# Two graph layers on one core: layer 0's T built transposed and unnormalized, its four second-set PSUM banks made one tile

## The chip, the cores and the metric

The kernel runs on one core of a Trainium2 chip. All data are fp32. The metric is the device time of one execution in microseconds. Engines are called PE (TensorE), DVE (VectorE), ACT (ScalarE), POOL (GpSimd) and SP (SyncE, which here only issues DMAs).

## The reference

Two layers work on 128 graphs of 128 nodes with 512 features. Layer 0, for each graph, with h = relu(layernorm(x)):

```python
Xw = X @ Wv + bv
sj = Xw @ aw[:d, 0]
si = Xw @ aw[d:, 0]
e = leaky_relu(sj[:, None, :] + si[:, :, None] + ab[0], negative_slope=0.2)
alpha_matrix = A * exp(e)
transition = alpha_matrix / (sum(alpha_matrix, axis=-1, keepdims=True) + 1e-12)
H = zeros; Xk = X
for k in range(3):
    H = H + Xk @ Wk[k] + bk[k]
    Xk = einsum('bij,bjd->bid', transition, Xk)
return relu(H)          # x = x + this
```

The kernel writes this as H = Y0 + T (Y1 + T Y2), with Yk = X Wk and T the transition matrix of the graph.

Layer 1, again on relu(layernorm(x)), forms q and k by one weight matrix, agg = adj k, a score per node from q and agg, a softmax of the scores over the nodes, and adds the softmax times X Wv1 to x.

## The kernel before, in words

**Pairs.** Layer 0 treats two graphs at a time (G = 2): 64 pairs p. The two graphs are the two block rows of one Strassen-Winograd product, so each product X W of a pair takes seven block products (`strassen`, L361) instead of eight. They run in the order P1, P5, P6, P2, P7, P3, P4, each of two accumulating matmuls, on four PSUM banks a, b, c, e. ACT copies one bank into another to seed the next accumulation (b<-a after P1, c<-b after P6) or into a buffer s (after P5 and P7). DVE adds s to a bank for the results e + s and b + s.

**Two bank sets.** PSUM has eight banks, each a tile of its own (L79): set1 = a1, b1, c1, e1, set2 = a2, b2, c2, e2 (L81). `y10` (L501) works on set1 and forms [Y1 | Y0] of pair p with 512 columns per matmul. `y2` (L427) works on set2 and forms Y2 of pair p + 2 with 257 columns, of which one is an attention column (si or sj).

**One pair in the loop (L644).** PE's order is written by hand: `ordered` (L88) chains every matmul to the one before. It is y10(p); inside it, after P6, two transposes of T(p) into a2 (`t_transposed`, L482); then `inner` (L514), four matmuls of 256 columns that add T Y2 onto the Y1 halves of the four set1 banks, each followed by an ACT copy of the sum to zz; then `outer` (L524), four matmuls of 256 columns that add T times that onto the Y0 halves; then y2(p + 2). DVE finishes with max(bank, 0) + x for each of the four blocks (L533), which goes to DRAM as x1d.

**T.** `attention` (L453) builds, on DVE and ACT, z = exp(leaky relu(sums of the two columns)), multiplies by the adjacency tile ag with a row sum (L466), adds 1e-12, takes the reciprocal and scales (L472). ag is loaded by SP (L107). A second copy of the adjacency matrix, agb, is loaded blockwise by POOL (L111) and transposed on DVE to aT (L475), times the mask, for layer 1.

**What else shares the queues.** For layer 1, DVE transposes h2 (`for_layer1`, L403) and, in every second pair, forms four sums (L420 to L424) that POOL's queue writes out (L422, L425). POOL's queue also carries the small pzd and pz DMAs of `y2` (L443, L445). `norm0`, `begin` and `norm2` make the layernorms and the left factors of coming pairs; `norm2_statistics(p)` runs behind product 2 of y2(p + 2).

**Order on the other engines.** A framework derives the waits between engines from the tiles that instructions read and write, and places DVE's, ACT's, POOL's and SP's instructions by its own plan of the times. `behind` (L83) keeps an instruction from being placed before a named earlier one.

**Layer 1** (L705 on) works on quads of four graphs, 32 in all. `together` (L809) alternates: product i on set1, product i on set2, product i + 1 on set1, and so on, with 2 + 2 factors and then 2 + 1; four matmuls on a1, a2, e1, e2 for `aggregate` (L879) stand in between. Its evacuations are like those of layer 0 (`one_round`, L741; `plain_ends`, `adding_ends`).

Of the kernel before, what the change touches and what calls it, by code (L numbers as in the profile page):

```python
# [16 lines left out]
def kernel(  # L17
# [60 lines left out]

    a1, b1, c1, e1, a2, b2, c2, e2 = (psum.tile([P, D], FP, name=n) for n in  # L79
                                      ("a1", "b1", "c1", "e1", "a2", "b2", "c2", "e2"))  # L80
    set1, set2 = (a1, b1, c1, e1), (a2, b2, c2, e2)  # L81
# [14 lines left out]

    xg, ag, agb = {}, {}, {}

# [4 lines left out]
    def load_adj(p):  # L103

        s = slice(p * G, (p + 1) * G)
        ag[p] = loads.tile([P, G, N], FP, name="ag", bufs=3)
        nc.sync.dma_start(ag[p], adj[s].rearrange("b n m -> n b m"))  # L107
        agb[p] = loads.tile([P, G, Q, S32], FP, name="agb", bufs=2)
        v = adj[s].rearrange("g (q b) (c i) -> c b (g q) i", b=S32, i=S32)
        for c in range(Q):  # L110
            nc.gpsimd.dma_start(agb[p][c * S32:(c + 1) * S32].rearrange("p g q i -> p (g q) i"), v[c])  # L111
# [21 lines left out]
    wkt = setup.tile([P, DC, D], FP, name="wkt")  # L133
    aw_bc = setup.tile([P, 2, D], FP, name="aw_bc")
    awr = t10[0:1, 2].rearrange("p c o -> p (c o)")
# [86 lines left out]
    def attention_columns():  # L222

        for f in range(DC):
            for a in range(2):
                junk = front.tile([P, D], FP, name="junk", bufs=1)
                done["u"] = nc.vector.scalar_tensor_tensor(
                    junk, wv0_sb[:, f], 1.0, aw_bc[:, a, :], op0=OP.mult, op1=OP.mult, accum_out=r2[:, f, a * (W2 + HD):a * (W2 + HD) + 1]).ins

# [81 lines left out]

    HV, LEFT, Y2, PZ, T, TT, X1, HV2, FW = ({} for _ in range(9))

# [89 lines left out]
    def for_layer1(p):  # L403

        q, second = divmod(p, 2)
        if not second:
            FW[q] = left.tile([P, 8, G, HC, N], FP, name="fw")
        f = FW[q]
        blocks, hv = f[:, L21:SLOT[4] + 1] if second else f[:, 0:SLOT[2] + 1:2], HV2.pop(p)
        for j in range(G):  # L410
            for k in range(2):
                nc.vector.transpose(blocks[:, k, j].rearrange("p f (n b) -> p f n b", n=Q),
                                    hv[:, j].rearrange("p n (k f a) -> p k f n a", k=2, f=HC)[:, k])
        if second:
# [9 lines left out]
            done["c12"] = nc.vector.tensor_sub(at[3], at[2], at[6]).ins  # L424
            queue.dma_start(fd[:, 4:].rearrange("p o n -> p (o n)"), fv[:, 4:].rearrange("p o n -> p (o n)"))  # L425

    def y2(p, steps={}, gate=None):  # L427


        add = partial(behind, gate, nc.vector.tensor_add) if gate else nc.vector.tensor_add  # L430
        y = Y2[p] = front.tile([P, G, 2, WP], FP, name="y2")[:, :, :, :W2]
        s = front.tile([P, 2, WP * 2], FP, name="s", bufs=1)[:, :, :W2]
# [20 lines left out]
    def attention(p, early_work=None):  # L453

        a, y, pz = ag.pop(p), Y2[p], PZ.pop(p)
# [8 lines left out]
        d = small.tile([P, 2, G], FP, name="d")  # L464
        for j in range(G):
            nc.vector.scalar_tensor_tensor(z[:, j, :], z[:, j, :], 1.0, a[:, j, :], op0=OP.mult,  # L466
                                           op1=OP.mult, accum_out=d[:, 0, j:j + 1])
        nc.vector.tensor_scalar(d[:, 0], d[:, 0], 1e-12, None, op0=OP.add)
        nc.vector.reciprocal(d[:, 1], d[:, 0])
        t = T[p] = front.tile([P, G, N], FP, name="t", bufs=1)  # L470
        for j in range(G):
            done["t"] = nc.vector.tensor_scalar(t[:, j, :], z[:, j, :], d[:, 1, j:j + 1], None,  # L472
                                                op0=OP.mult).ins
        aT = front.tile([P, G, N], FP, name="aT", bufs=1)
        nc.vector.transpose(aT.rearrange("p g n -> p (g n)"),  # L475
                            agb.pop(p).rearrange("p g q i -> p (g q i)"))
        for j in range(G):
            b = p * G + j
            behind("z", nc.scalar.activation, aT[:, j, :], aT[:, j, :], AF.Copy, scale=maskT[:, b:b + 1])
        nc.sync.dma_start(ATD[p], aT)  # L480

    def t_transposed(p):  # L482

        t, tt = T.pop(p), front.tile([P, G, N], FP, name="tt", bufs=1)
        pt = a2[:, :G * N].rearrange("p (g n) -> p g n", g=G)
        for j in range(G):
            ordered(nc.tensor.transpose, pt[:, j, :], t[:, j, :], ident)
        nc.scalar.copy(tt, pt)
        TT[p] = tt

# [7 lines left out]

    blocks1 = [(0, 0, a1), (1, 1, e1), (0, 1, b1), (1, 0, c1)]

    def y10(p, steps):  # L501

        s = front.tile([P, 2, WP * 2], FP, name="s", bufs=1)[:, :, :D]

        def end12(b, t):
            done["c12"] = behind("rs" if p else "t", nc.vector.tensor_add, b, b, t).ins

        strassen(set1, LEFT.pop(p), right10, s, False, {
            (0, 0): lambda a: None,
            (1, 1): lambda e, t: behind("rs" if p else "t", nc.vector.tensor_add, e, e, t),  # L510
            (0, 1): end12,
            (1, 0): lambda c: None}, steps, "warm" if p else "z")

    def inner(p):  # L514

        y = Y2.pop(p)
        z = front.tile([P, G, 2, HD], FP, name="zz", bufs=1)
        for j, nh, bank in blocks1:
            ordered(nc.tensor.matmul, bank[:, :HD], TT[p][:, j, :], y[:, j, nh, 1 - nh:W2 - nh], start=False,
                    stop=True, skip_group_check=True)  # L520
            nc.scalar.copy(z[:, j, nh], bank[:, :HD])
        return z

    def outer(p, z):  # L524

        tt, xs = TT.pop(p), xg.pop(p)
        hb = X1[p] = front.tile([P, G, D], FP, name="x1")
        for j, nh, bank in blocks1:
            ordered(nc.tensor.matmul, bank[:, HD:], tt[:, j, :], z[:, j, nh], start=False, stop=True,
                    skip_group_check=True)  # L530
        for j, nh, bank in blocks1:
            at = slice(nh * HD, (nh + 1) * HD)
            done["x1"] = nc.vector.scalar_tensor_tensor(hb[:, j, at], bank[:, HD:], 0.0, xs[:, j, at],  # L533
                                                        OP.max, OP.add).ins
        nc.sync.dma_start(X1D[p].rearrange("g n d -> n g d"), hb)
# [108 lines left out]
    for p in range(NP):  # L644
# [16 lines left out]
        if p > 1:  # L661
            behind("rs2", attention, p)
        y10(p, {1: between, 6: lambda: t_transposed(p)})
        if p > 0:
# [29 lines left out]
        if p == 3 + len(FACTORS):  # L694
# [415 lines left out]
```

## Time and profile before

| | us |
|---|---|
| median of 3 runs | 2298.38 |
| fastest, slowest of them | 2295.79, 2299.22 |
| span of the profiled execution | 2296.6 |
| layer 0 with its start, about | 0 to 1488 |
| layer 1, about | 1488 to 2296.6 |
| one pair of layer 0 (half of 687.96 to 732.51) | 22.27 |

The profile gives the span of the profiled execution, from its first to its last instruction; no other time of that execution is given, and the median lies 1.8 us above the span. In the timeline a line has the start in us, the length in us, the engine, the source line, the operation, what it writes and reads, and how many instructions are merged into it; in brackets stands how long the engine was idle before and what ended that. One fp32 matmul of the program appears as two MATMUL records, and their ends are modelled and overlap the next start, so that the distance between starts is what one takes. PEld is the weight load that goes ahead of a matmul.

### The profile page before, as it was taken

The numbers are of one execution on the slowest core, as the hardware profiler recorded it, in microseconds if no ns is written. First come the engines' busy times: TensorE is split into PE (matmuls) and PEld (weight loads), VectorE is DVE, ScalarE is ACT, GpSimd is POOL, SyncE is SP. The second block draws the span as 40 slices with busy tenths as digits, with TensorE's granted clock in tenths as the row PEclk, the third lists the DMA queues.
The fourth block names the chain that finished last, engine by engine and source line by source line (L and its number), as shares of the span: only waits on it lengthen the run. The fifth ranks groups of instructions, "written<-read, shape, count | busy, mean of one in ns | idle before, by whom it ended". The sixth has DMA issues, their size and how long they took to land.

```text
span 2296.6 us, 28967 instructions
## 1 busy us (share of the span) xinstructions
PE 2234.1 (97%) x8227; PEld 1547.1 (67%) x8227; DVE 1625.1 (71%) x4463; ACT 1273.3 (55%) x2933; POOL 699.6 (30%) x827
## 2 busy tenths in 40 slices
PE   9899999999999999999999999999999999999997
PEld 5565656566666656666565666578888888888885
DVE  5677767777677677767767776567777776776777
ACT  4455545555555555555555555356666666666665
POOL 3012111211212121121212112135555555555554
PEclk9999999999999999999999999999999999999999
DMA  8587786766766666676666667567888888888886
GB/s 228 161 261 218 240 243 212 219 211 195 237 200 213 223 208 214 196 236 197 211 228 203 217 198 224 186 242 225 246 234 231 240 231 229 249 232 231 246 237 190
DMA packets 343503, 507.78 MB, mean 221 GB/s; under 512 B 33178, under 2 KB 198426, under 8 KB 326958
## 3 DMA queue, kind: packets, MB, share of 16 engines
q1 hardware_dynamic: 302060, 382.40, 52.5%
q0 software_dynamic: 40992, 123.00, 20.1%
q8 instruction: 65, 1.06, 0.2%
q14 instruction: 96, 0.79, 0.1%
q10 hardware_dynamic: 290, 0.53, 0.1%
HBM read 289.62 MB, written 216.18 MB: 220 GB/s over the span
## 4 chain that ended last, share of the span: by engine, by line
PE 84%; DVE 6%; DMA 4%; ACT 4%; issue 2%; SPq 0%; POOL 0%; DVEq 0%; ACTq 0%; POOLq 0%
PE a L91 26%; PE c L91 23%; PE b L91 21%; PE e L91 13%; ACT h L306 2%; DVE z L466 1%; DMA rw<-rwd 1%; ACT s L86 1%; DMA pw<-pwd 1%; DMA h2d<-h 1%; DMA hd<-h 0%; DMA pwd<-pwt 0%; ACT z L463 0%; DMA tl<-in_L_gnn_Wqk_dram 0%; DVE t L472 0%
## 5 line engine op out<-in xcount | busy, mean ns | idle before, releaser
L111 POOL DMA_DIRECT2D agb<-in_adj_dram x256 | 150.2, 591 | 543.0 <-DVE aT L475 521.5
L570 POOL TENSOR_TENSOR c<-s,c 128x512 f32<-128x512 f32 (+1 forms) x186 | 199.7, 1088 | 257.9 <-DVE s L570 253.1
L91 PE MATMUL a<-r,x 128*128 128x512 f32 x512 | 243.4, 598 | 3.3 <-ACT a L493 3.2
L91 PE MATMUL b<-rw,in 128*128 128x256 f32 x896 | 215.0, 379 | 0.0
L91 PEld LDWEIGHTS b<-rw,in 128*128 128x128 f32 x896 | 170.6, 190 | 23.3
L289 DVE TENSOR_TENSOR r<-r 128x2 f32<-128x2 f32 x128 | 20.6, 161 | 214.6 <-ACT r L288 214.6
L386 ACT COPY s<-c 128x257 f32<-128x257 f32 (+1 forms) x128 | 61.4, 480 | 188.0 <-PE c L91 187.9
L570 POOL TENSOR_TENSOR c<-c 128x1024 f32<-128x1024 f32 (+1 forms) x70 | 152.2, 2184 | 13.6 <-DVE c L570 13.3
L91 PEld LDWEIGHTS a<-r,x 128*128 128x128 f32 x512 | 94.3, 195 | 68.9 <-issue 62.0
L378 ACT COPY b<-a 128x257 f32<-128x257 f32 (+1 forms) x128 | 59.4, 464 | 133.7 <-PE a L91 132.8
L91 PE MATMUL a<-w,x 128*128 128x257 f32 x512 | 132.0, 380 | 1.0 <-DVE x L338 1.0
L91 PE MATMUL b<-w,sx 128*128 128x257 f32 x512 | 132.0, 380 | 0.0
L443 POOL DMA_DIRECT2D pzd<-pzt x62 | 36.9, 595 | 281.4 <-DVE pzt L86 275.7
L91 PE MATMUL b<-t,sx 128*128 128x512 f32 x256 | 120.5, 593 | 1.0 <-ACT b L378 1.0
L91 PE MATMUL c<-t,x 128*128 128x512 f32 x256 | 120.4, 593 | 1.1 <-ACT s L386 1.1
L91 PE MATMUL c<-t,sx 128*128 128x512 f32 x256 | 121.3, 597 | 0.0
L91 PE MATMUL e<-t,sx 128*128 128x512 f32 x256 | 121.3, 596 | 0.0
L91 PE MATMUL b<-r,sx 128*128 128x512 f32 x256 | 120.3, 592 | 0.0
L570 DVE SCALAR_TENSOR_TENSOR junk<-agg,wscale,c 128x512 f32<-128x512 f32 x128 | 97.9, 765 | 31.4 <-POOL c L570 25.8
L570 ACT ACTIVATE c<-c,wcol 128x512 f32<-128x512 f32 x125 | 87.1, 719 | 59.4 <-DVE wcol L570 57.7
L306 ACT ACTIVATE h<-xg,rs 128x512 f32<-128x512 f32 x128 | 97.2, 807 | 37.5 <-DVE rs L294 36.5
L91 PE MATMUL c<-rw,in 128*128 128x256 f32 x448 | 109.1, 383 | 2.7 <-ACT c L570 2.6
(248 smaller groups left out, 5296.0 us busy)
## 6 DMA issues: line engine op xcount, KB each, us to landing
fd<-fw POOLq DMA_DIRECT2D x62, 1024.0 KB, 6.9
x1d<-x SPq DMA_DIRECT2D x64, 512.0 KB, 3.6
h2d<-h SPq DMA_DIRECT2D x64, 512.0 KB, 2.9
hv<-h2d SPq DMA_DIRECT2D x256, 128.0 KB, 4.3
f<-fd SPq DMA_DIRECT2D x32, 1024.0 KB, 6.1
xg<-in_x_dram SPq DMA_DIRECT2D x63, 512.0 KB, 4.8
hd<-h SPq DMA_DIRECT2D x63, 512.0 KB, 2.8
hv<-hd SPq DMA_DIRECT2D x252, 128.0 KB, 3.2
```

Source lines behind the costliest of these rows:

```text
L86: return op(*args, **how)
L91: done["mm"] = op(*args, **how).ins
L111: nc.gpsimd.dma_start(agb[p][c * S32:(c + 1) * S32].rearrange("p g q i -> p (g q) i"), v[c])
L289: nc.vector.tensor_mul(r[:, 2], r[:, 1], r[:, 1])
L306: nc.scalar.activation(to, at, AF.Relu, bias=rs[:, 1, j:j + 1], scale=rs[:, 0, j:j + 1])
L378: nc.scalar.copy(b, a)
L386: done["s7"] = nc.scalar.copy(s[:, 1], c).ins
L443: nc.gpsimd.dma_start(d.rearrange("g q b -> q g b"), t[::S32])
L466: nc.vector.scalar_tensor_tensor(z[:, j, :], z[:, j, :], 1.0, a[:, j, :], op0=OP.mult, op1=OP.mult, accum_out=d[:, 0, j:j + 1])
L570: done[engine] = op(*args, **how).ins
```

## The change

- The four banks of set2 become slices of one tile `banks2` of four banks. set1 stays four tiles.
- T is built transposed and without division: t = z times aT on DVE, directly in the layout that a matmul needs. The adjacency tile ag, its DMA, `t_transposed` with its two PE transposes and the ACT copy of T are gone. The attention columns of Y2 swap their places for it (index 1 - a).
- Y2 lies in two fixed buffers filled with ones at the start. The 257th column in front of `inner` is such a column of ones, so that T Y2 brings the row sums with it.
- `inner` writes to set2, starts new sums there, and stands behind P7 of y10 instead of behind P4.
- y10's four results go to a buffer yk in SBUF, by ACT copies for (0,0) and (1,0), which before stayed in PSUM, and by the DVE adds.
- `denominators` (DVE, two small operations) takes the row sums out of PSUM; `inner_out` (DVE, two operations of 512) divides T Y2 and adds Y1.
- `outer` is two matmuls of 512 columns to b1 and c1. u = bank / sum + Y0 is made by DVE, relu by ACT, the addition of x by POOL.
- The sums for layer 1 become a step of their own behind u. agb has three buffers, `stage` one.

```diff
-    a1, b1, c1, e1, a2, b2, c2, e2 = (psum.tile([P, D], FP, name=n) for n in
-                                      ("a1", "b1", "c1", "e1", "a2", "b2", "c2", "e2"))
+    a1, b1, c1, e1 = (psum.tile([P, D], FP, name=n) for n in ("a1", "b1", "c1", "e1"))
+    banks2 = psum.tile([P, 4, D], FP, name="banks2")
+    a2, b2, c2, e2 = (banks2[:, i] for i in range(4))
     set1, set2 = (a1, b1, c1, e1), (a2, b2, c2, e2)
...
-        ag[p] = loads.tile([P, G, N], FP, name="ag", bufs=3)
-        nc.sync.dma_start(ag[p], adj[s].rearrange("b n m -> n b m"))
-        agb[p] = loads.tile([P, G, Q, S32], FP, name="agb", bufs=2)
+        agb[p] = loads.tile([P, G, Q, S32], FP, name="agb", bufs=3)
...
+    y2s = [wpool.tile([P, G, 2, WP], FP, name=f"y2_{i}") for i in range(2)]
+    for t in y2s:
+        nc.gpsimd.memset(t, 1.0)
...
-        for j in range(G):
-            nc.vector.scalar_tensor_tensor(z[:, j, :], z[:, j, :], 1.0, a[:, j, :], op0=OP.mult,
-                                           op1=OP.mult, accum_out=d[:, 0, j:j + 1])
-        nc.vector.tensor_scalar(d[:, 0], d[:, 0], 1e-12, None, op0=OP.add)
-        nc.vector.reciprocal(d[:, 1], d[:, 0])
-        t = T[p] = front.tile([P, G, N], FP, name="t", bufs=1)
-        for j in range(G):
-            done["t"] = nc.vector.tensor_scalar(t[:, j, :], z[:, j, :], d[:, 1, j:j + 1], None,
-                                                op0=OP.mult).ins
...
+        t = TT[p] = front.tile([P, G, N], FP, name="t")
+        done["t"] = nc.vector.tensor_mul(t, z, aT).ins
...
-        for j in range(G):
-            ordered(nc.tensor.transpose, pt[:, j, :], t[:, j, :], ident)
-        nc.scalar.copy(tt, pt)
...
+        def add(j, nh, bank, t):
+            done["c12"] = behind(gate, nc.vector.tensor_add, to(j, nh), both(bank), both(t)).ins
+            if nh == j:
+                behind("c12", denominators, p)
+
+        strassen(set1, LEFT.pop(p), right10, s, False, {
+            (0, 0): lambda a: nc.scalar.copy(to(0, 0), both(a)),
+            (1, 1): partial(add, 1, 1),
+            (0, 1): partial(add, 0, 1),
+            (1, 0): lambda c: nc.scalar.copy(to(1, 0), both(c))}, steps, "warm" if p else "z")
+
+    def inner(p):
+
+        Y2.pop(p)
+        y = y2s[p % 2].rearrange("p j h o -> p (j h o)")
+        for i in range(4):
+            j, nh = divmod(i, 2)
+            n = D if p == NP - 1 and i in (1, 2) else W2
+            at = i * WP + 1 - nh
+            ordered(nc.tensor.matmul, set2[i][:, :n], TT[p][:, j, :], y[:, at:at + n], start=True, stop=True)
+
+    def denominators(p):
+
+        d = DEN[p] = small.tile([P, 2, G], FP, name="d")
+        nc.vector.tensor_scalar(d[:, 0], banks2[:, 0::2, HD], 1e-12, None, op0=OP.add)
+        nc.vector.reciprocal(d[:, 1], d[:, 0])
+
+    def inner_out(p):
+
+        z = Z[p] = y2s[p % 2][:, :, :, :HD]
+        for j in range(G):
+            done["c12"] = nc.vector.scalar_tensor_tensor(z[:, j], banks2[:, 2 * j:2 * j + 2, :HD], DEN[p][:, 1, j:j + 1],
+                                           yk[:, j, 0], op0=OP.mult, op1=OP.add).ins
...
+        for j, bank in enumerate((b1, c1)):
+            ordered(nc.tensor.matmul, bank.rearrange("p (h o) -> p h o", h=2), tt[:, j, :], z[:, j], start=True, stop=True)
+        us = [yk[:, j, 1].rearrange("p h o -> p (h o)") for j in range(G)]
+        for j, (u, bank) in enumerate(zip(us, (b1, c1))):
+            done["u0"] = nc.vector.scalar_tensor_tensor(u, bank, d[:, 1, j:j + 1], u, op0=OP.mult, op1=OP.add).ins
+            nc.scalar.activation(u, u, AF.Relu)
+            done["x1"] = nc.gpsimd.tensor_add(hb[:, j], u, xs[:, j]).ins
...
-        y10(p, {1: between, 6: lambda: t_transposed(p)})
+        y10(p, {1: between, 7: lambda: inner(p)})
+        behind("c12", inner_out, p)
...
-        z = inner(p)
...
-        behind("c12" if p else "left", outer, p, z)
+        behind("c12" if p else "left", outer, p)
+        if p > 0:
+            behind("u0", sums_for_layer1, p - 1)
...
-            stage = stage_ctx.enter_context(tc.tile_pool(name="stage", bufs=2, side="right"))
+            stage = stage_ctx.enter_context(tc.tile_pool(name="stage", bufs=1, side="right"))
```

More of the change, by code (lines that the diff above doesn't have):

```diff
@@ L95, in bcast @@
         return bass.AP(tensor=ap.tensor, offset=ap.offset + offset, ap=[[0, P], [1, n]])
-    xg, ag, agb = {}, {}, {}
+    xg, agb = {}, {}
     def load_x(p, queue=nc.sync):
@@ L133 @@
     wkt = setup.tile([P, DC, D], FP, name="wkt")
-    aw_bc = setup.tile([P, 2, D], FP, name="aw_bc")
+    yk = wpool.tile([P, G, 2, 2, HD], FP, name="yk")
+    aw_bc = yk[:, 0].rearrange("p k h o -> p k (h o)")
+    junk = yk[:, 1, 0].rearrange("p h o -> p (h o)")
     awr = t10[0:1, 2].rearrange("p c o -> p (c o)")
@@ L225, in attention_columns @@
             for a in range(2):
-                junk = front.tile([P, D], FP, name="junk", bufs=1)
                 done["u"] = nc.vector.scalar_tensor_tensor(
-                    junk, wv0_sb[:, f], 1.0, aw_bc[:, a, :], op0=OP.mult, op1=OP.mult, accum_out=r2[:, f, a * (W2 + HD):a * (W2 + HD) + 1]).ins
+                    junk, wv0_sb[:, f], 1.0, aw_bc[:, a, :], op0=OP.mult, op1=OP.mult, accum_out=r2[:, f, (1 - a) * (W2 + HD):(1 - a) * (W2 + HD) + 1]).ins
     def attention_constant():
@@ L310, in unpermuted @@
         return h.rearrange("p (f c a) -> p c f a", c=DC, f=Q)
-    HV, LEFT, Y2, PZ, T, TT, X1, HV2, FW = ({} for _ in range(9))
+    HV, LEFT, Y2, PZ, TT, DEN, Z, X1, HV2, FW = ({} for _ in range(10))
+    y2s = [wpool.tile([P, G, 2, WP], FP, name=f"y2_{i}") for i in range(2)]
+    for t in y2s:
+        nc.gpsimd.memset(t, 1.0)
     H2D, ATD, X1D = ([dram.tile(shape, FP, name=f"{name}{p}", bufs=1) for p in range(NP)]
@@ L413, in for_layer1, with sums_for_layer1 @@
                                     hv[:, j].rearrange("p n (k f a) -> p k f n a", k=2, f=HC)[:, k])
+    def sums_for_layer1(p):
+        q, second = divmod(p, 2)
         if second:
@@ L423, in for_layer1 @@
             nc.vector.tensor_sub(at[7], at[1], fv[:, L21])
-            done["c12"] = nc.vector.tensor_sub(at[3], at[2], at[6]).ins
+            nc.vector.tensor_sub(at[3], at[2], at[6])
             queue.dma_start(fd[:, 4:].rearrange("p o n -> p (o n)"), fv[:, 4:].rearrange("p o n -> p (o n)"))
@@ L430, in y2 @@
         add = partial(behind, gate, nc.vector.tensor_add) if gate else nc.vector.tensor_add
-        y = Y2[p] = front.tile([P, G, 2, WP], FP, name="y2")[:, :, :, :W2]
+        y = Y2[p] = y2s[p % 2][:, :, :, :W2]
         s = front.tile([P, 2, WP * 2], FP, name="s", bufs=1)[:, :, :W2]
@@ L453, in attention @@
     def attention(p, early_work=None):
-        a, y, pz = ag.pop(p), Y2[p], PZ.pop(p)
+        y, pz = Y2[p], PZ.pop(p)
         z = front.tile([P, G, N], FP, name="z", bufs=1)
@@ L463, in attention @@
         done["z"] = nc.scalar.activation(z, z, AF.Exp).ins
-        d = small.tile([P, 2, G], FP, name="d")
-        for j in range(G):
-            nc.vector.scalar_tensor_tensor(z[:, j, :], z[:, j, :], 1.0, a[:, j, :], op0=OP.mult,
-                                           op1=OP.mult, accum_out=d[:, 0, j:j + 1])
-        nc.vector.tensor_scalar(d[:, 0], d[:, 0], 1e-12, None, op0=OP.add)
-        nc.vector.reciprocal(d[:, 1], d[:, 0])
-        t = T[p] = front.tile([P, G, N], FP, name="t", bufs=1)
-        for j in range(G):
-            done["t"] = nc.vector.tensor_scalar(t[:, j, :], z[:, j, :], d[:, 1, j:j + 1], None,
-                                                op0=OP.mult).ins
         aT = front.tile([P, G, N], FP, name="aT", bufs=1)
@@ L480, in attention @@
         nc.sync.dma_start(ATD[p], aT)
-    def t_transposed(p):
-        t, tt = T.pop(p), front.tile([P, G, N], FP, name="tt", bufs=1)
-        pt = a2[:, :G * N].rearrange("p (g n) -> p g n", g=G)
-        for j in range(G):
-            ordered(nc.tensor.transpose, pt[:, j, :], t[:, j, :], ident)
-        nc.scalar.copy(tt, pt)
-        TT[p] = tt
     def seed_a():
@@ L497, in seed_e, with to, both @@
         nc.scalar.copy(e1, bias_e.rearrange("p k o -> p (k o)"))
-    blocks1 = [(0, 0, a1), (1, 1, e1), (0, 1, b1), (1, 0, c1)]
     def y10(p, steps):
         s = front.tile([P, 2, WP * 2], FP, name="s", bufs=1)[:, :, :D]
-        def end12(b, t):
-            done["c12"] = behind("rs" if p else "t", nc.vector.tensor_add, b, b, t).ins
+        gate = "rs" if p else "t"
+        def to(j, nh):
+            return yk[:, j, :, nh]
+        def both(bank):
+            return bank.rearrange("p (k o) -> p k o", k=2)
@@ L508, in y10 @@
+        def add(j, nh, bank, t):
+            done["c12"] = behind(gate, nc.vector.tensor_add, to(j, nh), both(bank), both(t)).ins
+            if nh == j:
+                behind("c12", denominators, p)
         strassen(set1, LEFT.pop(p), right10, s, False, {
[L509 to L512, printed above, removed]
+            (0, 0): lambda a: nc.scalar.copy(to(0, 0), both(a)),
+            (1, 1): partial(add, 1, 1),
+            (0, 1): partial(add, 0, 1),
+            (1, 0): lambda c: nc.scalar.copy(to(1, 0), both(c))}, steps, "warm" if p else "z")
@@ L514, in inner @@
     def inner(p):
[L516 to L526, printed above, removed]
-        hb = X1[p] = front.tile([P, G, D], FP, name="x1")
[L528 to L534, printed above, removed]
+        Y2.pop(p)
@@ new lines, in inner_out, with outer @@
+    def inner_out(p):
[3 more added lines that the diff above has]
+                                           yk[:, j, 0], op0=OP.mult, op1=OP.add).ins
+    def outer(p):
+        tt, xs, d, z = TT.pop(p), xg.pop(p), DEN.pop(p), Z.pop(p)
+        hb = X1[p] = front.tile([P, G, D], FP, name="x1")
+        for j, bank in enumerate((b1, c1)):
[5 more added lines that the diff above has]
+            done["x1"] = nc.gpsimd.tensor_add(hb[:, j], u, xs[:, j]).ins
@@ L680 @@
         if p == 0:
-            behind("x1", norm0, 3)
+            behind("u0", norm0, 3)
             setup_ctx.close()
@@ L702 @@
     for_layer1(NP - 1)
+    sums_for_layer1(NP - 1)
     def left1(q, o, i):
```

## The prediction, written before the changed kernel was run

> **What bounds the kernel now.** I read the page's engine shares first, then the chain that ended last, then two stage windows, then the timeline of one pair.
>
> ```profile
> span 2296.6 us, 28967 instructions
> PE 2234.1 (97%) x8227; PEld 1547.1 (67%) x8227; DVE 1625.1 (71%) x4463; ACT 1273.3 (55%) x2933; POOL 699.6 (30%) x827
> PE 84%; DVE 6%; DMA 4%; ACT 4%; issue 2%; SPq 0%; POOL 0%; DVEq 0%; ACTq 0%; POOLq 0%
> ```
>
> TensorE is the bound, and the stage windows (two pairs of layer 0; two quads of layer 1) say how tightly:
>
> ```profile
> core 0: us, PE busy (x) PEld busy (x) DVE busy (x) ACT busy (x) POOL busy (x), PEclk, DMA share, GB/s
> 687.96:732.51 44.55, 43.83 (x150) 27.61 (x149) 31.71 (x103) 23.86 (x56) 8.13 (x14) 1.00 0.68 212
> 1666.00:1715.67 49.67, 49.67 (x216) 40.71 (x215) 36.50 (x72) 31.34 (x70) 27.59 (x23) 1.00 0.81 234
> ```
>
> A pair of layer 0 takes 22.27 us with about 0.35 us of it idle on PE, a quad of layer 1 24.5 us with none. So whatever makes PE wait is added in full. Why it hardly waits today is seen in the timeline of one second-set product, Y2:
>
> ```profile
> 707.99 1.03 PE L91 MATMUL a<-w,x 128*128 128x257 f32 x4
> 708.86 1.03 PE L91 MATMUL e<-w,sx 128*128 128x257 f32 x4
> 709.05 0.36 ACT L378 COPY b<-a 128x257 f32<-128x257 f32 x1 [2.22 <-PE a L91]
> 709.72 1.03 PE L91 MATMUL b<-w,sx 128*128 128x257 f32 x4
> ```
>
> Products start 0.867 us apart. The copy out of bank a starts 0.19 us after P1's slot ended and lies wholly under the product into bank e. The one steady stall is at the transposes that the change removes:
>
> ```profile
> 720.09 0.52 PE L91 MATMUL a<-ident,t 128*128 128x128 f32 x2 [0.72 <-DVE t L472]
> 720.45 1.88 PE L91 MATMUL a<-r,x 128*128 128x512 f32 x4
> ```
>
> The two transposes hold PE for 0.36 us (720.09 to 720.45); over the kernel the list of waits counts 26.3 us in 31 waits of PE for t.
>
> **What the Trainium skill says.** "PSUM — Partial Sum Buffer", section "PSUM bank collisions raise a hardware error", asks that PSUM be guarded by bank and quadrant, and says that accesses to different banks run clean; so a wait between different banks is not asked for by the chip. "Perfetto Trace Analysis", section "Matmuls", wants matmul groups to rotate through banks so that the evacuation of one overlaps the next group; the four lines above agree (copy at 709.05 to 709.41 under 708.86 to 709.72). "TensorE: Matmul & The Clock Gate", section on the clock gate, says that an idle PE drops to half clock; the trace agrees once: after a wait of 3.20 us at 1468.58 two 512-wide products took 2.50 and 2.73 us instead of 1.72. Waits of 0.98 and 1.59 us early in the trace were followed by full-speed products.
>
> **The decisive edit: one tile for four banks.** The second set becomes slices of one tile `banks2`. I compared the two built programs instruction by instruction, with the semaphores that each waits for. In before, Y2's seven products wait for an evacuation three times (P6, P7, P4), each with a product in between as cover. In after, P5, P6, P2, P7, P3 and P4 all wait, each for the copy or add that reads the bank written just before it, though their own bank is another:
>
> ```
> product, bank     after waits for           before waits for
> P5  e2            ACT copy b2<-a2           nothing
> P6  b2            ACT copy s<-e2            ACT copy b2<-a2
> P2  a2            ACT copy c2<-b2           nothing
> P7  c2            ACT copy y<-a2            ACT copy c2<-b2
> P3  b2            DVE add y<-e2,s           nothing
> P4  c2            DVE add y<-b2,s           ACT copy s<-c2
> ```
>
> Nothing lies between product and evacuation any more. The price of such a wait is in before's start-up, where ACT was late once:
>
> ```profile
> 31.99 0.34 ACT L378 COPY b<-a 128x257 f32<-128x257 f32 x1
> 32.38 1.13 PE L91 MATMUL b<-w,sx 128*128 128x257 f32 x4
> 33.35 1.03 PE L91 MATMUL a<-w,x 128*128 128x257 f32 x4
> 33.55 0.36 ACT L86 COPY c<-b 128x257 f32<-128x257 f32 x1 [0.65 <-PE b L91]
> ```
>
> The copy ends at 32.33, PE starts 0.05 later, the product takes 0.97 (33.35 - 32.38, its weights no longer loaded ahead), ACT starts 0.20 after. One step is 0.97 + 0.20 + 0.36 + 0.05 = 1.58 us instead of 0.867: +0.71.
>
> **One pair of layer 0, step by step**, zero at the end of y10's last product P4.
> 1. Removed: transposes 0.36, and the stall of about 0.34 (22.27 less 14 x 0.86 + 14 x 0.4335 + 8 x 0.4325 + 0.36 = 21.93).
> 2. `inner` keeps its PE time (4 x 0.43) and moves behind P7; T is made by DVE well before, so no wait.
> 3. `outer`, 2 x 0.86 for 4 x 0.43: equal. But its second product needs ACT's copy of c1 (0.20 + 0.58), then the division (a 128x512 DVE operation with PSUM; nearest row 0.70): ready at 1.60 with 0.05 per handover, while the first product ends at 0.86. With 0.10 for exposed weights it ends at 2.56, not 1.72: +0.84.
> 4. Y2 from 2.56. P1 to 3.43. P5 to 5.01. Between these copies ACT, in order, has two new Relus (0.76 each, by the row of h), so the copy of e2 ends at 5.90. P6 5.95 to 6.92, P2 7.53 to 8.50, P7 9.11 to 10.08, copy of c2 to 10.66. P3 needs a DVE add of 0.42 behind the statistics of x1, which now wait for DVE, ACT and two POOL adds (1.09 each): add at 10.7 to 11.0. P3 11.2 or 11.5 to 12.2 or 12.4, P4 to 14.0 or 14.1. Y2 takes 11.45 for 6.07: +5.4.
> 5. y10's P7 waits for ACT's copy c1<-b1. In every second pair ACT has the two h activations ahead of it, and these wait for statistics that DVE starts only after T, the transposes and sx: I get the copy at 22.3 against P7 due at 21.0, so +1.5 there, 0.75 on average.
> 6. Beside PE: DVE loses the two masks with sums, t and four x1 pieces (about 3.2) and gains one multiply, two divisions and two u (about 3.6); POOL gains 2 x 1.09 in a queue that also issues agb, pz and fd; SP loses the ag load. In a pair of 28 us none of them is full, so I cost them at nothing outside the chain of step 4. If POOL's queue holds them up, Ln is later, up to 0.5.
>
> Sum: -0.36 - 0.34 + 0.84 + 5.4 + 0.75 = +6.3 a pair; 62 pairs with a Y2: +390. Y2 of the first two pairs: about +5 each, 10. The last two pairs, without Y2, I leave at zero.
>
> **Layer 1.** Here the sets alternate, so a set-1 product (0.86) covers each evacuation. Copies (0.20 + 0.57) just fit: 0 to 0.1 each. P3 doesn't fit: P7, copy 0.20 + 0.59, DVE add 0.69, 0.05 is 1.53 against 0.86, so about 0.8 with exposed weights, twice a quad. P4 of the second half stands behind two adds and a small multiply of DVE:
>
> ```profile
> 1713.53 1.02 DVE L570 TENSOR_TENSOR s<-e,s 128x512 f32<-128x512 f32 x2 [0.65 <-ACT s L570]
> 1714.67 0.98 DVE L570 TENSOR_TENSOR wcol<-wcol 128x4 f32<-128x4 f32 x1
> 1715.58 1.01 DVE L570 TENSOR_TENSOR s<-b,s 128x512 f32<-128x512 f32 x2
> ```
>
> P4 was due at 15.24 and the second add ends at 16.59: 0.3 to 1.0 after the earlier delays. P6 there waits behind an exp on ACT: 0.5. Eight small ones of 0.1 to 0.2. Sum 3.8 a quad, bounds 2 and 5; 31.5 quads: +120 (63 to 158).
>
> **Total** 2296.6 + 390 + 10 + 120 = 2817 of span; the median of the runs lies 1.8 above the profiled span; the page gives no other time for that execution. With some slack taken off step 5, which rests on an order of ACT that could come out milder, I say 2805.
>
> **Unknowns, from both sides.** Division and u read two PSUM banks or strided halves, forms the trace lacks: 0.41 x 2 bounds them above, 0.6 below; 0.70 taken. Step 5: 0 to 3 us in every second pair: -46 to +46. Layer 1 as above.
>
> **Rivals.**
> - Clock. PE is idle for nearly half of Y2, though never over 1.5 us at once. If that already lowers the clock through half of each Y2, 3 us more a pair: about 2990. For: the slow products after 3.20 us. Against: full speed after 0.98 and 1.59.
> - Milder: the copies overlap better than one by one, and layer 1's alternation hides nearly all: Y2 +3.5, step 5 zero, layer 1 +40: 62 x 3.6 + 10 + 40, about 2575.
> - Not slower: only waits on the same bank cost time. Then layer 1 is unchanged and the pair keeps gains of up to 0.36 x 64 + 43 (all of PE's idle time between 36.9 and 1487 us, 1450.1 less 1406.8) = 66 against 0.84 x 64 = 54: about 2286. It decides where the six waits cost under 0.03 us each (12 / (62 x 6)). Against: the program has them, and the start-up shows 0.71 for one.
>
> **Chances.** Forecast 0.74, clock 0.11, milder 0.09, not slower 0.06. The forecast's own range is 2690 to 2900; for 8 in 10 I reach half way to the clock case and a little to the milder one: 2660 to 2930. Changes under 0.2% (some 5 us) can't be told from none. Faster 0.04, same 0.02, slower 0.94.
>
> **What would show it.** Right: in the changed kernel each Y2 product starts about 1.6 us after the last, with "ACT" or "DVE" named before PE; P1 to P4 starts about 10.5 us apart; PE's busy share near 80%; a wait before outer's second product near 0.75; no transposes from T; second-set P3 in layer 1 late by 0.7. Wrong: Y2 products still 0.867 apart, or PEclk under 9 in the slices.

## The result and the profile after

| | before | after |
|---|---|---|
| median of 4 runs, us | 2297.09 | 2841.60 |
| fastest, slowest | 2295.47, 2299.22 | 2839.07, 2847.05 |
| span of the profiled execution, us | 2296.6 | 2840.8 |
| mean granted TensorE clock in it | 0.995 | 0.973 |
| a pair of layer 0, mean of 36 in the middle, us | 22.27 | 29.20 |

The changed kernel takes 1.2376 times as long (95% interval 1.2358 to 1.2394): 544.5 us more. The pairs are counted from the start of y10's first product: 413.89 to 1464.97 in after is 36 pairs.

The page of after has these three lines for the three that were shown of before:

```profile
span 2840.8 us, 27824 instructions
PE 2477.2 (87%) x7843; PEld 1446.0 (51%) x7843; DVE 1776.4 (63%) x4143; ACT 1322.4 (47%) x2869; POOL 895.3 (32%) x957
PE 61%; DVE 22%; ACT 8%; issue 5%; DMA 2%; POOL 2%; SPq 0%; DVEq 0%; ACTq 0%; POOLq 0%
```

PE went from 97% busy to 87%, and DVE and ACT from 10% of the chain that ended last to 30%; the copies and adds that empty PSUM are done by these two engines. PE's busy time went up by 243 us for fewer instructions: the records themselves are longer (1.13 for 1.03 us behind a wait, up to 2.88 below), so "87%" flatters PE (the prediction had looked for 80%). The stage window says it more plainly (two pairs of after; idle is 9.23 us of 58.51):

```profile
core 0: us, PE busy (x) PEld busy (x) DVE busy (x) ACT busy (x) POOL busy (x), PEclk, DMA share, GB/s
927.74:986.25 58.51, 49.28 (x137) 25.23 (x136) 35.15 (x93) 25.17 (x54) 14.18 (x18) 0.97 0.52 161
```

And the timeline of PE at one pair, from outer's first product to the second product of the next y10:

```profile
925.17 1.12 PE L92 MATMUL b<-y,t 128*128 128x512 f32 x2
926.78 1.13 PE L92 MATMUL c<-y,t 128*128 128x512 f32 x2 [0.48 <-DVE y L532]
927.74 1.03 PE L92 MATMUL banks<-w,x 128*128 128x257 f32 x4
929.22 1.14 PE L92 MATMUL banks<-w,sx 128*128 128x257 f32 x4 [0.45 <-ACT banks L382]
930.87 1.13 PE L92 MATMUL banks<-w,sx 128*128 128x257 f32 x4 [0.52 <-ACT s L87]
932.51 1.13 PE L92 MATMUL banks<-w,x 128*128 128x257 f32 x4 [0.50 <-ACT banks L87]
934.20 1.13 PE L92 MATMUL banks<-w,sx 128*128 128x257 f32 x4 [0.56 <-ACT y L442]
936.43 1.14 PE L92 MATMUL banks<-w,sx 128*128 128x257 f32 x4 [1.10 <-DVE y L87]
938.08 1.87 PE L92 MATMUL banks<-w,x 128*128 128x257 f32 x4 [0.52 <-DVE y L87]
939.75 2.88 PE L92 MATMUL a<-r,x 128*128 128x512 f32 x4
942.46 1.88 PE L92 MATMUL e<-t,sx 128*128 128x512 f32 x4
```

Where products of Y2 stood 0.867 us apart, they stand 1.48 to 2.23 apart, each but the first with an ACT or DVE instruction named that has just emptied another bank. P4 and the product after it show a second thing: P4 needs 1.67 us to the next start (938.08 to 939.75) instead of 0.97, and the first 512-wide product 2.71 (939.75 to 942.46) instead of 1.72. That is a stretch at half clock (the last section shows the granted clock of this stretch, 0.50). The 40 slices of the page don't show it: PEclk is 9 in all of them, before and after.

### The profile page after: what moved, and what is told of

Same layout as the page of the kernel before. It is cut to its first block, busy times and chain, and to the rows that moved or that the text cites. A ratio compares the mean times of both kernels' runs of the same rounds, so it can differ in the third digit from the quotient of the medians.

```text
span 2840.8 us, 27824 instructions
## 1 busy us (share of the span) xinstructions
PE 2477.2 (87%) x7843; PEld 1446.0 (51%) x7843; DVE 1776.4 (63%) x4143; ACT 1322.4 (47%) x2869; POOL 895.3 (32%) x957
## 4 chain that ended last, share of the span: by engine, by line
PE 61%; DVE 22%; ACT 8%; issue 5%; DMA 2%; POOL 2%; SPq 0%; DVEq 0%; ACTq 0%; POOLq 0%
PE banks L92 24%; PE c L92 12%; PE a L92 11%; PE b L92 8%; PE e L92 6%; DVE s L581 3%; DVE st L282 2%; POOL x L545 2%; DVE fw L429 2%; DVE y L87 2%; ACT h L306 2%; DVE fw L416 1%; DVE yk L543 1%; ACT yk L510 1%; ACT s L581 1%
## 5 line engine op out<-in xcount | busy, mean ns | idle before, releaser
L545 POOL TENSOR_TENSOR x<-yk,xg 128x512 f32<-128x512 f32 x128 | 193.7, 1529 | 854.3 <-ACT yk L544 814.9
L92 PE MATMUL banks<-w,sx 128*128 128x257 f32 x1024 | 297.0, 413 | 182.7 <-DVE y L87 80.7
L92 PEld LDWEIGHTS banks<-w,sx 128*128 128x128 f32 x1024 | 176.5, 192 | 300.6 <-DVE y L87 105.7
L92 PE MATMUL banks<-w,x 128*128 128x257 f32 x768 | 233.1, 430 | 68.3 <-ACT banks L87 32.9
L92 PE MATMUL banks<-rw,in 128*128 128x256 f32 x768 | 227.4, 405 | 33.2 <-DVE s L581 18.8
L92 PEld LDWEIGHTS banks<-w,x 128*128 128x128 f32 x768 | 144.7, 202 | 166.8 <-DVE y L87 59.5
L92 PEld LDWEIGHTS banks<-rw,in 128*128 128x128 f32 x768 | 130.3, 189 | 110.4 <-DVE s L581 47.4
L532 DVE SCALAR_TENSOR_TENSOR y<-banks,d,yk 128x512 f32<-128x512 f32 x128 | 96.1, 751 | 57.0 <-ACT yk L510 54.8
L92 PE MATMUL banks<-y,t 128*128 128x257 f32 x512 | 125.0, 387 | 2.9 <-DVE t L476 2.9
L92 PEld LDWEIGHTS banks<-y,t 128*128 128x128 f32 x512 | 98.1, 192 | 46.3 <-issue 30.8
```

The source lines that it names most:

```text
L92: done["mm"] = op(*args, **how).ins
L532: done["c12"] = nc.vector.scalar_tensor_tensor(z[:, j], banks2[:, 2 * j:2 * j + 2, :HD], DEN[p][:, 1, j:j + 1], yk[:, j, 0], op0=OP.mult, ...
L545: done["x1"] = nc.gpsimd.tensor_add(hb[:, j], u, xs[:, j]).ins
```

## The experiments

Eleven versions are told here, each with what was written down before it ran; there is no e4. "A pair" is always the mean over 36 pairs in the middle of layer 0. All times are medians of 4 runs, beside 7 runs of before (medians 2295.2 to 2297.9 us) on the same chip.

### e1: the one tile undone

```diff
-    banks2 = psum.tile([P, 4, D], FP, name="banks2")
-    a2, b2, c2, e2 = (banks2[:, i] for i in range(4))
+    a2, b2, c2, e2 = (psum.tile([P, D], FP, name=n) for n in ("a2", "b2", "c2", "e2"))
...
-        nc.vector.tensor_scalar(d[:, 0], banks2[:, 0::2, HD], 1e-12, None, op0=OP.add)
+        for j, bank in enumerate((a2, c2)):
+            nc.vector.tensor_scalar(d[:, 0, j:j + 1], bank[:, HD:W2], 1e-12, None, op0=OP.add)
```

`inner_out` is likewise written bank by bank.

> Kernel after, but the second set is again four tiles of one bank each; the row sums and the division, which read two banks at once, become one operation per bank (2 + 4 small ones for 1 + 2). All else of the change stays. Theory (the one tile costs nearly everything): Y2's products are 0.87 us apart again and layer 1 is as before; of the rest of the change only the removed transposes and stall (-0.70 a pair) and the wait before the second product of outer (+0.85 to +1.0 a pair, one division operation more in the chain) remain: 62 x 0.15 to 0.3 = +9 to +19, so 2290 to 2320 us. Rival (the rest of the change, with two Relus more on ACT and two adds of 128x512 on POOL, is itself slow): 2500 us or more, with waits of PE for the second set's adds left in the trace.

Measured: 2395.56 us, ratio 1.0432 (1.0416 to 1.0447), a pair 23.96. Y2's products are 0.867 us apart again, and the granted clock is back at 0.992:

```profile
883.02 1.03 PE L91 MATMUL a<-w,x 128*128 128x257 f32 x4
883.89 1.03 PE L91 MATMUL e<-w,sx 128*128 128x257 f32 x4
```

The one tile is worth 2841.6 - 2395.6 = 446 of the 544 us. The theory was right on that and wrong on the rest: the other parts of the change cost 99 us, 1.69 a pair and not 0.15 to 0.3. Where they lie is told with e6 to e9.

### e2: the one tile alone, put into the kernel before

```diff
-    a1, b1, c1, e1, a2, b2, c2, e2 = (psum.tile([P, D], FP, name=n) for n in
-                                      ("a1", "b1", "c1", "e1", "a2", "b2", "c2", "e2"))
+    a1, b1, c1, e1 = (psum.tile([P, D], FP, name=n) for n in ("a1", "b1", "c1", "e1"))
+    banks2 = psum.tile([P, 4, D], FP, name="banks2")
+    a2, b2, c2, e2 = (banks2[:, i] for i in range(4))
```

> Kernel before, in which only the second set becomes one tile of four banks. The built program has the same six waits in Y2 as the kernel after. Theory: six steps of up to 1.58 for 0.87 us, +4.3 a pair, 62 x 4.3 = 267, the first two Y2 +10, layer 1 +113 (3.6 a quad, as the kernel after shows it): about 2690 us, 2620 to 2760. What is missing to 2841 us, about 150, is then the part that the new Relus and POOL adds make worse by lying ahead of the copies and the statistics. Rival 1 (only waits on the same bank cost time): 2297. Rival 2 (Relus and POOL adds do not matter, the one tile is the whole loss): 2830 or more.

Measured: 2682.86 us, ratio 1.1687 (1.1667 to 1.1706), a pair 26.74, clock 0.996. These three lines, which don't change a single operation of the computation, cost 386 us; the theory gave 390. So the cause holds from both sides. Y2 takes 11.08 us here. The 159 us by which e2 falls short of after were put down to the Relus and POOL adds beforehand; e10, which takes both out of after, does not get them back.

### e3: the one tile in layer 0 only

```diff
     layer0.close()
+    psum0.close()
+    psum1 = ctx.enter_context(tc.tile_pool(name="psum1", bufs=1, space=bass.MemoryType.PSUM))
+    a2, b2, c2, e2 = (psum1.tile([P, D], FP, name=n) for n in ("a2", "b2", "c2", "e2"))
+    set2 = (a2, b2, c2, e2)
```

> Kernel after with the one tile in layer 0 alone: it is given up at the end of layer 0, and layer 1 gets four tiles of one bank. Theory: layer 1 is back at 24.5 us a quad instead of 28.1, 31.5 x 3.6 = 113 us less: 2728 us, 2700 to 2745. Rival (layer 1's losses come from layer 0's late products or from the lower granted clock, not from the tile): 2800 or more.

Measured: 2738.70 us, ratio 1.1924 (1.1901 to 1.1947). Layer 1's share is 103 us, 3.3 a quad. In after, its worst wait is that of the second set's P3 (start, length, engine, what it waits for):

```profile
2330.73 1.03 PE L92 MATMUL b<-rw,in 128*128 128x256 f32 x4
2332.30 1.13 PE L92 MATMUL banks<-rw,in 128*128 128x256 f32 x4 [0.54 <-DVE s L581]
```

The product of the first set (into b1) covers the copy of P7 but not copy and add: 2330.73 to 2332.30 is 1.57 us for a product of 0.86, so P3 is 0.71 late.

### e5: two tiles of two banks

```diff
+    ab2, ce2 = (psum.tile([P, 2, D], FP, name=n) for n in ("ab2", "ce2"))
+    a2, b2, c2, e2 = ab2[:, 0], ab2[:, 1], ce2[:, 0], ce2[:, 1]
```

> Kernel after with two tiles of two banks, a2 with b2 and c2 with e2, so that the division still reads two banks at once. Built, Y2 keeps only P2 waiting at once for the copy c2<-b2, and P4 waiting for the add out of e2 with P3 between. Theory: P2 +0.71, P4 +0.2 to 0.5, the wait of outer +0.75, transposes and stall -0.70, so about +1.1 a pair = 68; layer 1 one wait of this kind a half, +10 to +40: 2365 to 2420 us. Rival (the number of waits does not matter, the first one already shifts ACT and DVE so that all are late): 2550 or more.

Measured: 2531.94 us, ratio 1.1028 (1.1008 to 1.1047), a pair 25.67. The theory missed by over 100 us; the rival is nearer, and not met either. P2 costs what it should (0.50 idle, 34.8 us in 64 waits), but P4, which has a whole product as cover, waits most (PE's list of waits: total, times, longest):

```profile
PE ce L92 <- DVE y L87: 132.6, 62, 3.0
PE ab L92 <- ACT ce L87: 34.8, 64, 2.5
```

It waits for the DVE add into y(1,1), and DVE's timeline shows where that stood in the queue:

```profile
901.21 1.78 DVE L429 TENSOR_TENSOR fw<-fw 128x512 f32<-128x512 f32 x1
902.91 0.68 DVE L282 BATCH_NORM_STATS2 st<-x 128x6 f32<-128x512 f32 x1
...
906.97 0.16 DVE L294 SCALAR_TENSOR_TENSOR rs<-mv,rs 128x2 f32<-128x2 f32 x1
907.05 0.42 DVE L87 TENSOR_TENSOR y<-ce,s 128x257 f32<-128x257 f32 x1
```

The add comes behind the statistics of x1 (the argument "rs2" of y2 holds it there by hand), which come behind POOL's adds and the sums for layer 1. An evacuation that nobody waited for in before may stand anywhere in a queue; with a false wait behind it, its place in the queue is the cost. My expectation had priced the add and not the queue.

### e6 and e9: two orders on DVE

e6 is e1 with the four divisions held in their order a, b, c, e. e9 is e6 with the sums for layer 1 held behind the statistics of x1. The diff of e6 against e1, then that of e9 against e6:

```diff
-                done["c12"] = nc.vector.scalar_tensor_tensor(z[:, j, nh], ...
+                done["c12"] = behind("c12", nc.vector.scalar_tensor_tensor, z[:, j, nh], ...
```

```diff
-        if p > 0:
+        if p > 0 and p + 2 >= NP:
             behind("u0", sums_for_layer1, p - 1)
...
-            y2(p + 2, {2: partial(norm2_statistics, p)}, "rs2")
+            def statistics_first():
+                norm2_statistics(p)
+                if p > 0:
+                    behind("rs2", sums_for_layer1, p - 1)
+
+            y2(p + 2, {2: statistics_first}, "rs2")
```

> Kernel of the four tiles, with one more thing fixed: the four division operations are held in the order a, b, c, e. In e1 they ran as a, b, e, c, and in every second pair a transpose for layer 1 that waited for its DMA stood between e and c, so that the second product of outer waited 1.36 us instead of 0.22. Theory: the waits of PE for y at outer go from 34 us to 62 x 0.25 = 15, so 2396 - 19 = about 2377 us (2365 to 2385). Rival (that wait is only replaced by the copy b1<-a1 coming later still): 2392 or more.

> e6 (four tiles, Relu on ACT, x added by POOL) with one change of order: the sums for layer 1 are held behind the statistics of x1, so that on DVE three of the four 512-wide sums no longer stand ahead of them and none runs beside the POOL adds. Theory (the chain POOL adds beside DVE sums, then statistics, h, copy b1<-a1): the POOL adds of a second pair take 2.5 us instead of 3.3, the statistics come about 2 us earlier, the waits of PE for b1<-a1 (29.5 us) and for the copy to s (33.4) go to under 10 each, those for y stay: 2405 - 45 = about 2360 us (2340 to 2375). Rival (it is the length of the two POOL adds alone, whatever DVE does): 2390 to 2405.

Measured: e6 2405.10 us, ratio 1.0465 (1.0443 to 1.0487); e9 2398.71, ratio 1.0445 (1.0425 to 1.0465); a pair 23.96 and 23.95, in e1 23.96. Both theories fell, and both times lie in the range of the rival. e6 did not do to its own wait what it should: the wait before outer's second product became even, 0.70 us in 53 pairs, where e1 has 0.22 in 31 pairs and up to 2.3 in others, but its sum went from 34.0 us to 38.3 and not to 15. PE's waits in e6, and in e9:

```profile
PE c L91 <- DVE y L86: 38.3, 55, 0.7
PE c L91 <- ACT s L389: 33.4, 29, 1.4
PE b L91 <- ACT b L381: 29.5, 28, 1.3
```

```profile
PE c L91 <- ACT s L389: 63.2, 59, 1.4
```

In e9 POOL's two adds of a second pair take 2.5 us instead of 3.5, so the rival's reason, the length of these adds alone, is not borne out either. The waits for b1<-a1 are gone; but now P4 of every Y2 waits 1.1 us for the copy s<-c2, which ACT has behind the Ln of x1's statistics:

```profile
915.45 0.29 ACT L86 ACTIVATE r<-mv,eps 128x2 f32<-128x2 f32 x1 [1.56 <-DVE mv L282]
915.77 0.20 ACT L287 ACTIVATE r<-r 128x2 f32<-128x2 f32 x1
915.88 0.36 ACT L389 COPY s<-c 128x257 f32<-128x257 f32 x1
```

In both orders ACT stands still until the statistics of x1 are there, and some copy behind it is late.

### e7: x1 made by DVE

On top of e6:

```diff
-            nc.scalar.activation(u, u, AF.Relu)
-            done["x1"] = nc.gpsimd.tensor_add(hb[:, j], u, xs[:, j]).ins
+            done["x1"] = nc.vector.scalar_tensor_tensor(hb[:, j], u, 0.0, xs[:, j], OP.max, OP.add).ins
```

> e6 with the ACT Relu and the POOL add of each half of x1 replaced by one DVE operation max(u, 0) + x. Theory: what e1 still lost at P6 of y10 (36.7 us in 28 waits for the ACT copy b1<-a1) is a chain: in every second pair the two POOL adds take 3.3 us while the sums for layer 1 on DVE beside them take 1.8 us each instead of 0.7, so the statistics of x1, the two h activations and, behind them in ACT's order, the copy b1<-a1 are late. Without POOL adds the chain is 2 to 3 us shorter and the waits at P6 and at Y2's P4 (12 us) go: 2377 - 45 = about 2332 us (2315 to 2350). Rival (it is ACT's and DVE's amount of work, not the POOL adds): DVE has 1.4 us a pair more, no gain, 2375 or more.

Measured: 2323.22 us, ratio 1.0120 (1.0104 to 1.0136), a pair 22.59: 82 us less than e6, where 45 had been expected. DVE's busy time rises by 17 us (1750.0 to 1767.1), and both ACT copies are out of PE's list but for 1.6 us:

```profile
PE c L91 <- DVE y L86: 39.3, 56, 0.7
PE b L91 <- ACT b L381: 1.6, 2, 1.2
```

So what e1 lost beside outer's wait was the way DVE to ACT to POOL to DVE for x1, with POOL's adds at 1.46 us each (mean of 128 on the page of e1) and the statistics behind them. The Relu on ACT and the add on POOL went together; what each is worth alone no run shows. What is left is outer's own wait for the division, the first line.

### e8: outer's second product behind the first of Y2

On top of e7:

```diff
-            y2(p + 2, {2: partial(norm2_statistics, p)}, "rs2")
+            y2(p + 2, {2: partial(norm2_statistics, p), **({1: rest} if split else {})}, "rs2")
```

`rest` is the second half of outer, the sums for layer 1 and the load of x; `split` holds for pairs 1 to 61.

> e7 with the second product of outer moved behind the first product of Y2, so that 0.87 us of PE work cover the division of the second half (pairs 1 to 61). Theory: the wait of 0.22 us and the 0.24 lost around it disappear, 61 x 0.46 = 28 us: about 2304 us if e7 gives 2332 (28 less than e7 in any case; 20 to 35). Rival (x1 comes later by one product and the statistics with it, so that P4 of Y2 or P6 of y10 wait instead): no gain over e7, or a loss.

Measured: 2283.70 us, ratio 0.9948 (0.9933 to 0.9963), a pair 21.89: 39.5 us less than e7, where 20 to 35 had been expected, and 12.5 less than before. It is the one version that beats both kernels, before by 0.5%. Outer's wait is gone, and the window of one pair (columns as above) shows PE with hardly a gap:

```profile
919.19:941.04 21.85, 21.80 (x70) 12.85 (x68) 18.41 (x56) 12.12 (x27) 4.68 (x8) 1.00 0.78 252
```

A pair gains 22.27 - 21.89 = 0.38, 24 us in 62; about half of that is lost outside the steady pairs. Between 1470 and 1600 us, around the change of layers, PE is idle for 11.7 us; I have not followed that.

### e10, e11, e12: what the one tile makes of late statistics

Three edits to the kernel after, each alone, its one tile kept: x1 on DVE as in e7 (e10); outer split as in e8, but with the Relus and POOL adds (e11); and the statistics of x1 held behind Y2's two adds instead of ahead of them (e12, from whose diff this is):

```diff
-        add = partial(behind, gate, nc.vector.tensor_add) if gate else nc.vector.tensor_add
+        def add(*args):
+            done["y11"] = nc.vector.tensor_add(*args).ins
...
-            nc.vector.bn_stats(st, src[:, j, :])
+            behind(first, nc.vector.bn_stats, st, src[:, j, :])
```

> Kernel after with its one tile, and only the Relu and the POOL add of x1 replaced by one DVE operation as in e7. In the built program Y2's add into y(1,1) still stands behind the statistics of x1 on DVE, and P3 waits for it. Theory: the statistics come 2 to 3 us earlier, so P3's wait shrinks from 1.1 to 1.5 us towards 0.9, and the copies are no longer behind the Relus (P6, P2: 0.1 to 0.2 each): 0.7 to 1.2 us a pair, 2841 - 62 x 0.95 = about 2780 us (2740 to 2800). Rival (the loss of the one tile is all in the six handovers, with nothing lost to late statistics): 2830 to 2850.

> Kernel after with its one tile, and only the second product of outer moved behind the first product of Y2. Built, the first product of Y2 now waits for both divisions (they read the one tile), so the 0.48 us stays, but outer's second product lies between the copy b2<-a2 and P5 and covers it: 0.6 us a pair, 61 x 0.6 = 37. Theory 1 (the half clock at the end of Y2 in every second pair, about 50 us in all, is set off by how much PE idles in one Y2, 3.7 us of 12): with 3.2 us it goes or halves, 2841 - 37 - 25 to 50 = 2754 to 2780. Theory 2 (it is set off by the one long wait before P3): it stays, 2800 to 2808. Rival (x1 comes one product later and P3 waits that much longer): 2835 or more.

> Kernel after with its one tile, and one change of order on DVE: the two adds of Y2 are no longer held behind the statistics of x1, the statistics stand behind the adds instead. Theory 1 (P3's wait beyond the 0.93 us that the kernel before with one tile shows is this queue; the half clock comes from it): P3 waits 0.93 everywhere, 22 us less, and the half clock of every second pair goes, 50 us less. But the statistics, the h activations and the copy b1<-a1 behind them come later, and P6 of y10 waits about 1.3 us a pair for that copy, 80 us more: 2850 us (2820 to 2880), with a granted clock of 0.99. Theory 2 (the half clock is set off by the sum of the idle time in a pair, wherever it lies): the same waits, clock 0.97, about 2900. Rival (the statistics have slack): P6 does not wait, 2765 to 2790.

Measured:

| | us | ratio (95%) | clock | P3's wait, us | first y10 products over 1.9 us |
|---|---|---|---|---|---|
| after | 2841.6 | 1.2376 (1.2358 to 1.2394) | 0.973 | 1.10 or 1.48 | 29 |
| e10 | 2865.66 | 1.2481 (1.2463 to 1.2500) | 0.969 | 0.93 or 2.31 | 31 |
| e11 | 2924.38 | 1.2735 (1.2707 to 1.2763) | 0.944 | 1.10 or 3.23 | 51 |
| e12 | 2808.58 | 1.2209 (1.2177 to 1.2242) | 0.993 | 0.93 | 1 |
| e2 | 2682.86 | 1.1687 (1.1667 to 1.1706) | 0.996 | 0.93 | 1 |

e10 and e11 refute what I expected. x1 on DVE, which saves 82 us with four tiles, costs 24 with one. The split, which saved 39.5 us in e8, costs 83; but e8 had x1 on DVE and e11 has not, so these two do not show what the tile does to it. In e11 the rival came true: x1 comes one product later, and P3 waits the longer for it, 3.23 us in every second pair. About 42 of its 83 us are half clock: 50 pairs lose 92 us to it (28 pairs lose 50 in after), counted as P4 beyond 0.97 and y10's first product beyond 1.72; the table's last column has the start-up's slow product with them.

In e10 the place of Ln on ACT shows why (ACT, then DVE, of the same stretch):

```profile
977.47 0.37 ACT L390 COPY s<-banks 128x257 f32<-128x257 f32 x1 [1.22 <-PE banks L92]
977.74 0.30 ACT L87 ACTIVATE r<-mv,eps 128x2 f32<-128x2 f32 x1
```

```profile
978.30 0.16 DVE L289 TENSOR_TENSOR r<-r 128x2 f32<-128x2 f32 x1 [1.73 <-ACT r L288]
979.17 0.42 DVE L87 TENSOR_TENSOR y<-banks,s 128x257 f32<-128x257 f32 x1
```

In every second pair Ln stands behind the copy of P7's result, the statistics on DVE wait 1.73 us for it, and the add that P3 waits for stands behind the statistics: P3 pays for a chain over two engines. e12, which takes the add out of that chain, brings P3 down to 0.93 and the clock back to 0.993, and pays part of it back at P6 of y10, 0.83 us a pair:

```profile
960.66 1.88 PE L92 MATMUL e<-t,sx 128*128 128x512 f32 x4
963.37 1.99 PE L92 MATMUL b<-t,sx 128*128 128x512 f32 x4 [0.83 <-ACT b L382]
```

Of its three cases, e12 bears out the first in kind (the same waits, the same clock), with 33 us gained where 9 lost had been forecast.

## Why the prediction was right, point by point

**The decisive edit** held: six waits in each Y2, in the order and with the engines named beforehand; e1 and e2 show it from both sides, 446 and 386 us.

**One pair**, the steps of the prediction and what after shows:

| step | predicted | measured | from |
|---|---|---|---|
| 1 transposes and stall gone | -0.70 | -0.70 | P6 and P2 of y10 at 944.18 and 945.90, 1.72 apart with nothing between; no wait for t in the pairs |
| 3 outer's second product | +0.84 | +0.85 | 927.74 - 925.17 = 2.57, was 1.72 |
| 4 Y2 | +5.4 | +5.8 | mean 11.88 (33 of 11.57, 28 of 12.24), was 6.07 |
| 5 P7 of y10 | +0.75 | +0.28 | 948.19 - 945.90 = 2.29 for 1.72, in every second pair |
| clock, y10's first product | 0 | +0.52 | 31.7 us in 28 pairs, over 61 |
| sum | +6.3 | +6.76 | the pair itself: 29.20 - 22.27 = +6.93 |

**Step 4** came out as it was derived. P6 was put at 3.39 us after P1's start and stands at 3.13 (the two Relus take 1.15 us together, not 1.52); P3 at 8.64 to 8.94 and stands at 8.69 or 9.04, by turns; P4 starts 10.34 or 10.69 after P1 in most pairs, forecast about 10.5. (By the forecast's own steps P4 ends at 13.8 or 14.1; its 14.0 is 0.2 high, which is 0.1 on average.) Of the 5.8, 0.3 is P4 at half clock.

**Step 5** was too large: P7 waits 0.57 us more in every second pair, not 1.5. The mechanism, ACT late behind the h activations, is the right one (the copy c1<-b1 follows them without a gap):

```profile
946.14 1.52 ACT L306 ACTIVATE h<-xg,rs 128x512 f32<-128x512 f32 x2 [1.02 <-DVE rs L294]
947.57 0.57 ACT L87 COPY c<-b 128x512 f32<-128x512 f32 x1
```

In e12, in which the statistics of x1 come later, a wait of the same kind stands at P6, 0.83 in every pair.

**Step 6** failed as a general statement. Beside the waits of the one tile, the longer way of x1 over ACT and POOL was costed at nothing, or up to 0.5 a pair. With four tiles it costs 82 us (e6 to e7), 1.4 a pair. In after it seems hidden for the most part: PE is idle anyway, and the lateness of x1 appears as P3's wait beyond 0.93 us, which step 4 does contain. The total was right; but whoever had taken only the one tile back, trusting step 6, would have expected some 2306 (62 x 0.14 more than before) and got 2396.

**Layer 1**: forecast 120, measured 103 by e3. Its eight small waits and P6 behind the exp were not separated by a run.

**The rivals.** "Not slower" is refuted by e2. "Milder" too: layer 1 alone was to lose 40 us and lost 103, Y2 5.8 us and not 3.5. "Clock" happened in part: half clock for the last product of Y2 and the first of y10 in 28 of 61 pairs, 0.67 + 1.13 = 1.80 us each, 50 us, where the rival had 3 us in every pair. The forecast's own sum, 2817, lacks these 50 and has some 17 too many in layer 1 and 29 in step 5 (62 x 0.47). The 12 us then taken off step 5 for a milder order came true on that step, but they were outweighed by the clock; about 20 us of the 2840.8 are not placed. So 50 us missing and 46 too many nearly cancel, and that the 2805 came within 40 us of the result is in part luck; the size of Y2's step is not. The check "PEclk under 9" was too coarse to show the clock: a slice lasts 71 us and the half clock about 3. The prediction had also read too few cases: besides the wait of 3.20 us, the trace of before has half clock after waits of 4.45 (at 89.68), 3.05 (at 313.42) and 2.62 us (at 1537.90), and full clock after one of 2.49 (at 348.35).

## What to carry to other kernels

A tile is the unit in which this framework orders accesses: here four banks in one tile behaved like one bank, and a schedule that rotates through banks is lost without any operation changing. Before two banks are made one tile for the sake of one wide instruction, count the products that will wait for an evacuation next door; here three DVE operations per pair were saved (3 in place of the 6 of e1) at the price of 5.8 us. And cost every instruction that is newly waited for by its place in its engine's queue, not by its length: in e5 an add of 0.42 us cost a wait of 2.99, and x1 on DVE gained 82 us with four tiles (e7) and lost 24 with one (e10).

## What the runs showed of the hardware that was not expected

**Half clock without a long idle time.** The Trainium skill, "TensorE: Matmul & The Clock Gate", section "Part 1: The HAM clock gate", tells of a drop to half clock after an idle window of about 3.4 us, in windows that run freely; it also names frequent short idle times between groups of matmuls, without saying how much is too much. Here no single wait of PE in after's pairs is over 1.5 us, and it drops. With 3.4 us idle in a Y2 of 11.1 us it doesn't (e2 and e12, no drop in 61 pairs each; one pair of e2 has 4.5 us in 12.1), with 4.8 us in 13.3 it does each time (e10, 30 of 30), with 3.6 to 4.0 in about half of the pairs (after, 28 of 61). It is not the idle time of the whole pair: e12 has 0.83 us more at P6 and keeps full clock. Nor does one wait of 1.4 us between long products do it (e1).

So the sum of the idle time alone does not decide. The clock records of the traces show more. In all 13 traces each stretch at half clock, but for one cut off by the end, lasts one to four times 3.413 us, and within a trace all begin on one grid of this spacing, which agrees with windows that run freely. The pair shown above in three steps of this grid (columns as above; PE's busy time and PEclk are what matters):

```profile
934.92:938.33 3.41, 1.79 (x7) 0.93 (x7) 2.18 (x8) 2.09 (x4) 2.30 (x4) 1.00 0.58 195
938.33:941.74 3.41, 3.41 (x7) 2.02 (x7) 2.55 (x8) 1.07 (x3) 0.61 (x2) 0.50 0.67 220
941.74:945.15 3.41, 3.41 (x9) 1.50 (x9) 1.76 (x5) 1.56 (x4) 0.59 (x1) 1.00 0.52 120
```

A step in which PE was busy for 0.52 of the time is followed by one at half clock. I took the least busy step of each Y2 in the six runs with one tile in layer 0 (after, e2, e3, e10, e11, e12; 366 pairs): below 0.49 the clock always dropped, above 0.53 never, in between in some pairs. By the modelled ends of the matmuls no sharper line comes out, and it is not a rule for every kernel: in e5, with one long wait in place of several, a step at 0.42 kept the clock.

What decides in after is thus where the waits of a pair fall on the grid. Of the 30 pairs with P3's wait of 1.10 us, the 22 that dropped have P3 starting 1.27 to 1.51 or 2.99 to 3.33 us into a step, and none of the 8 others has. Two pairs last 58.06 us (413.89 to 471.96), almost exactly 17 steps (58.03), so that the same kind of pair meets the same place of the grid many times in a row; that is why, for long stretches, every second pair drops.

**POOL beside DVE.** "SBUF — State Buffer", section "SBUF: two separate sides", says that DVE with two SBUF inputs and GpSimd exclude each other on a shared port. The traces agree: a 512-wide DVE sum of two SBUF operands takes 1.61 us in e1, where it runs beside the POOL adds, and 0.72 in e9, where it doesn't (means of 32); the POOL add takes 1.46 and 1.30 (means of 128).
